# Two feed-forward couples of the last batch but one moved to the last steps, with other row buffers and new order seeds

## The chip, the cores and the metric

The kernel runs on one core of a Trainium2 chip. The metric is the device time of one execution in microseconds (us). The engines of a core are TensorE (PE, matrix products), VectorE (DVE), ScalarE (ACT), GpSimd (POOL) and SyncE (SP, which issues nearly all DMAs here). Each has its own queue and works through it in order; they wait for each other by semaphores.

## What is computed

One transformer block in float32 on x of shape (8, 1024, 256): attention with 16 heads of 64, then a feed-forward part, each with a layernorm before it and another behind it, ahead of the residual sum. Shortened from the reference:

```python
def attn(x):                       # x already normalised
    q, k, v = (einsum('btc,hcd->bhtd', x, W) for W in (Wq, Wk, Wv))
    scores = einsum('bhtd,bhsd->bhts', q, k) / sqrt(64) + bias   # bias by clipped distance, per head
    w = softmax(where(causal, scores, -inf))
    return concat_heads(einsum('bhts,bhsd->bhtd', w, v)) @ Wp + bp

def ffn(x):                        # x already normalised
    x_prev = shift_by_one_row(x)   # zero for the first row
    xr = mu_r * x + (1 - mu_r) * x_prev
    xk = mu_k * x + (1 - mu_k) * x_prev
    return sigmoid(xr @ W_r.T) * (square(relu(xk @ W_k.T)) @ W_v.T)

x = x + layernorm(attn(layernorm(x)))
x = x + layernorm(ffn(layernorm(x)))
```

## The kernel before, in words

**Tiling.** A batch has 1024 rows: eight tiles of 128, or four *couples* of 256 rows (c = 0 to 3). Heads go in pairs; a *unit* is one batch and one pair of heads, so there are 8 x 8 = 64 units (the unit u = 63 is the last). A unit takes four *steps*, 256 in all; a step makes the scores of two row tiles (`STEPS`: tiles 7 and 1, 6 and 0, 5 and 3, 4 and 2). The scores of tiles 4 to 7 ("long") are made in two parts, each in one of two slots `s` of PSUM; those of tiles 0 to 3 ("short") and all other products take one or two of four PSUM banks `pm`.

**The stages of attention.** `do_scores` (L1015): products of k and q in 64x64 tiles of the array (L1041), bias and maximum on DVE (L1070, L1078), exponentials on ACT (L1098), scaling of the probabilities p by the reciprocal of their sum on POOL (L1186). `turn` (L1197): DVE transposes p in 32x32 blocks into `blocks` (L1207); `shuffle` (L1260): sixteen DMAs on SP's queue bring the blocks to their places in `d`, once for each of a unit's two groups of row tiles. `do_av` (L1275): products of d and v (L1293); group 0 holds couples 3 and 0, group 1 couples 2 and 1; ACT saves them to `oT` (L1316). For the last tiles of unit 63 PE transposes p itself (`turn_by_pe`, L1221) and ACT and DVE copy it to d. `do_qk`, `do_v`: projections of the next unit, through the helper `matmul` (L433).

**The rows of a couple.** `stages_in` (L663) loads x rows (`xin`), normalises them (`xn`) and transposes them to `xnT`. `project_out` (L692) multiplies oT by Wp and adds to the rows `y`; `stages_out` (L737) loads the x rows once more (`xre`), normalises y and adds. `stages_ffn` (L752) is the feed-forward part: statistics on DVE (`norm_stats`, L516), normalised rows `yn` (`normed`, L532), transposition to `ynT`, the mixes `xk` and `xr` (one part on ACT, the other on DVE), the products xk by W_k, xr by W_r and ka by W_v (each eight matmuls of 256 columns, L433), relu and tanh on ACT, square, gate, layernorm, sum, store.

Transposition goes two ways. For all batches but the last, `by_dma` (L606): DVE transposes blocks into `st`, four DMAs bring them to DRAM (`via`), one brings them back into the rows' own buffer, ACT places them. In the last batch PE transposes (`turned`, L582), and normalisation and sums are done by ACT and DVE instead of POOL (`edge`).

**Buffers.** A `Ring` is a tag with n buffers; the n+1st owner waits until all users of the first are done. Before, `xin`, `xre`, `xn`, `yn`, `st`, `v` and the four `y{c}` have one buffer each. For batches other than the last, ka takes the ring of ynT.

**The order.** No engine's queue is written by hand. Every piece of work is a `Task` with an engine, a cost estimate, a priority and its dependences; `Planner.simulate` (L216) lists the tasks by priority, and each engine's instructions are emitted in that order. A task's priority is its step number (plus a fixed `RANK` for its kind, plus offsets drawn from a seed) times `STEP`. There are 65 `SEEDS` (L95), one for each stretch of 34 us of the planner's clock. Which work belongs to which step is set at the end of the kernel (L1451 to L1512): with end = the step at which a batch's attention ends, the next batch's rows enter at end - 15 + 2c, the out stages at end + 1 and following, and the feed-forward part of couple c at end + 6 + 3c. For batch 6 (the last but one) end is 224, so couples 2 and 3 enter at steps 236 and 239. The parts of the last batch enter at step LAST = 256.

Of the kernel before, what the change touches and what calls it, by code (L numbers as in the profile page):

```python
# [92 lines left out]

STRETCH = 34
SEEDS = (  # L95
    392905, 816692, 244547, 283470, 560662, 39100, 216772, 294259, 588279, 412218,
    371534, 0, 431774, 883409, 180062, 984965, 373709, 0, 0, 0,
    763639, 658110, 822178, 930278, 665013, 718545, 0, 952361, 100832, 846644,
    0, 137572, 647438, 377597, 0, 469262, 83528, 641677, 323164, 611824,
    444950, 813510, 452093, 622742, 919130, 335621, 0, 751616, 573689, 0,  # L100
    0, 99909, 466380, 402426, 0, 986219, 146830, 82811, 0, 0,
    151578, 369797, 955240, 0, 0,
)


# [47 lines left out]
class Planner:  # L153
# [13 lines left out]
    def add(  # L167
        self,
        eng,
        cost,  # L170
        fn,
        *deps,
        w=(),
        r=(),
        prio=0.0,
        mode="cols",
        banks=0,
        frees=None,
        mb=0.13,
    ):  # L180


        t = Task(eng, cost, fn, prio, mode, banks, mb)
        t.deps = list(deps)
        if self.gate is not None:
            t.deps.append(self.gate)
        for b in r:
            b, part = b if isinstance(b, tuple) else (b, None)
            t.deps += [d for p, d in b.writers if part is None or p == part]
            b.users.append(t)  # L190
        for b in w:
            b, part = b if isinstance(b, tuple) else (b, None)
            if b.maker is None:
                b.maker = t
                t.makes.append(b)
                if b.old is not None:
                    t.deps.append(b.old.users)
                if b.before is not None:
                    t.after.append(b.before.maker)
            elif b.maker is not t:  # L200
                t.after.append(b.maker)

            if frees is not None and b.old is not None:
                frees[0].deps.append(b.old.users)
            if frees is not None and b.maker is not t and (frees[0], 0) not in b.maker.frees:
                frees[0].after.append(b.maker)
            b.writers.append((part, t))
            b.users.append(t)
        if frees is not None:
            t.deps.append(frees[0])  # L210
            t.frees.append(frees)
            frees[0].readers[frees[1]] += 1
        self.tasks.append(t)
        return t
# [143 lines left out]
def tile_attn_ffn_block(  # L358
# [17 lines left out]
    B, T, C = x.shape  # L376
    H, _, D = Wq.shape
# [37 lines left out]
    ins = ctx.enter_context(tc.tile_pool(name="ins", bufs=1))  # L415
    acts = ctx.enter_context(tc.tile_pool(name="acts", bufs=1))
# [12 lines left out]
    def matmul(dst, lhs, rhs, first, last):  # L429
# [5 lines left out]
    rows2 = [P, 2, C]  # L435
    R = {
        "xin": Ring(ins, rows2, "xin", 1),
        "xre": Ring(ins, rows2, "xre", 1),
        "wq": Ring(ins, [P, NC, P], "wq", 1),
        "wk": Ring(ins, [P, NC, P], "wk", 1),  # L440
        "wv": Ring(ins, [P, 2, NC, D], "wv", 1),
        "xn": Ring(acts, rows2, "xn", 1),
        "st": Ring(acts, [P, NQ, 2 * NC, QD], "st", 1),
        "via": Ring(dram, [P, NQ, 2 * NC, QD], "via", 2),
        "yn": Ring(acts, rows2, "yn", 1),
        "xkr": Ring(acts, [P, NC, CT], "xkr", 1),
        "xr": Ring(acts, [P, NC, CT], "xr", 1),
        "ynT": Ring(acts, [P, NC, CT + 1], "ynT", 1),
# [15 lines left out]
        R[n, "long"] = Ring(small, [P, 2, 2], f"{n}_long", 3)  # L464
    for c in range(NCP):
        R["oT", c] = Ring(acts, [P, CT], f"oT{c}", HP + 1)
        R["y", c] = Ring(acts, rows2, f"y{c}", 1)
    for g in range(2):
        R["xnT", g] = Ring(acts, [P, NC, HB], f"xnT{g}", 2)


    def rows_of(t, b, c):
        return t[b, c * CT : (c + 1) * CT, :].rearrange("(n p) c -> p n c", p=P)
# [132 lines left out]
    def by_dma(dst, view, src, what, prio, last):  # L606


        st, via = R["st"](f"st_{what}"), R["via"](f"via_{what}")
        add(  # L610
            "dve",
            0.6,
            lambda: nc.vector.transpose(
                st.tile.rearrange("p r a j -> p a r j"),
                src.tile.rearrange("p k (c r j) -> p (k c) r j", r=NQ, j=QD),
            ),
            r=[src],
            w=[st],
            prio=prio,
        )  # L620


        def leave():
            v = via.tile
            n = 2 * NC * QD
            for q in range(NQ):
                nc.sync.dma_start(
                    bass.AP(
                        tensor=v.tensor,
                        offset=v.offset + q * n,  # L630
                        ap=[[NQ * n, QD], [QD * NQ * n, NQ], [1, n]],
                    ),
                    st.tile[q * QD : (q + 1) * QD],
                )

        def flat(t):
            return t.rearrange("p k f -> p (k f)")

        add("sp", NQ * ISSUE, leave, r=[st], w=[via], prio=prio, mb=0.26)
        add(  # L640
            "sp",
            ISSUE,
            lambda: nc.sync.dma_start(
                flat(src.tile), via.tile.rearrange("p q a j -> p (q a j)")
            ),
            r=[via],
            w=[src],
            prio=prio,
            mb=0.26,
        )  # L650

        def place():
            blks = flat(src.tile).rearrange("p (q k c j) -> p k q c j", k=2, c=NC, j=QD)
            for cc in range(NC):
                nc.scalar.copy(
                    view(dst.tile)[:, cc, :].rearrange("p (k q j) -> p k q j", k=2, j=QD),
                    blks[:, :, :, cc, :],
                )

        add("act", 0.7, place, r=[src], w=[dst], prio=last)  # L660
# [76 lines left out]
    def stages_out(b, c):  # L737


        def s0(prio):  # L740
            project_out(b, c, range(HP, NPAIR) if b < B - 1 else [NPAIR - 1], prio)
            rn = norm_stats(ys[b, c], f"ao_{b}_{c}", prio)
            xre = R["xre" if b < B - 1 else {0: "xre", 3: "xin", 1: "xn", 2: "xre"}[c]](
                f"xre_{b}_{c}"
            )
            load_rows(xre, b, c, prio)
            normed(ys[b, c], ys[b, c], rn, f"ao_{b}_{c}", prio + 1, edge=b == B - 1)
            plus(ys[b, c], xre, prio + 1, edge=b == B - 1)

        return [s0]  # L750

    def stages_ffn(b, c):  # L752

        box = {}

        def buf(name, tag, spare):

            if b < B - 1:
                return R[tag](f"{name}_{b}_{c}")
            return R[spare](  # L760
                f"{name}_{b}_{c}", lambda t: t[:, : NC * CT].rearrange("p (k f) -> p k f", k=NC)
            )
# [2 lines left out]
            box["rn"] = norm_stats(ys[b, c], f"y_{b}_{c}", prio)  # L765

        def s1(prio):
            box["yn"] = buf("yn", "yn", ("p", "short")) if c % 2 else R["yn"](f"yn_{b}_{c}")
            normed(box["yn"], ys[b, c], box["rn"], f"y_{b}_{c}", prio, edge=b == B - 1)

        def s2(prio):
# [557 lines left out]
    def start_lists(lists, prio, lag):  # L1329
        n = max(len(s) + i * lag for i, s in enumerate(lists))  # L1330
        for j in range(n):
            for i, s in enumerate(lists):
                if 0 <= j - i * lag < len(s):
                    s[j - i * lag](prio)
# [7 lines left out]
    with tc.tile_pool(name="prep", bufs=1) as prep:  # L1342
# [16 lines left out]
        for c in range(NCP):  # L1359
# [12 lines left out]
            prio=-4,  # L1372
# [6 lines left out]
            prio=-4,  # L1379
# [8 lines left out]
            prio=-1,  # L1388
# [16 lines left out]
        for half in range(2):  # L1405
# [7 lines left out]
            prio=2,  # L1413
# [30 lines left out]
    LAST = NU * NS  # L1444
    ahead = {}

    def later(step, stages):
        for i, s in enumerate(stages):
            ahead.setdefault(step + i, []).append(s)

    for b in range(B):  # L1451
        end = (b + 1) * NPAIR * NS
        mid = end - HP * NS
        for i, c in enumerate((0, 3, 1, 2)):
            later(mid + 3 + i, [lambda prio, b=b, c=c: project_out(b, c, range(HP), prio)])
        if b + 1 == B:
            for i, c in enumerate((0, 3, 1, 2)):
                later(
                    end - NS + i,
                    [lambda prio, b=b, c=c: project_out(b, c, range(HP, NPAIR - 1), prio)],  # L1460
                )
        else:
            for i, c in enumerate((0, 3, 1, 2)):
                later(end + 1 + 2 * i, stages_out(b, c))
            for c in range(NCP):
                ffn = stages_ffn(b, c)
                later(end + 6 + 3 * c, [lambda prio, ffn=ffn: start_lists([ffn], prio, 1)])
                later(end - 15 + 2 * c, stages_in(b + 1, c))

    for m in range(LAST):  # L1470
        u, st = divmod(m, NS)
# [34 lines left out]
    b = B - 1  # L1506
# [48 lines left out]
```

## Time and profile before

| | |
|---|---|
| three runs | 2192.37, 2194.66 and 3990.92 us; median 2194.66 |
| profiled execution | 2193.71 us, its span 2191.9 us |
| instructions in the span | 61295 |
| busy: PE | 2161.1 us |
| busy: DVE | 1970.5 us |
| busy: POOL | 1526.8 us |
| busy: ACT | 1377.4 us |
| DMA: read from HBM, written to HBM | 59.91 MB, 25.29 MB |
| mean granted TensorE clock | 0.998 |

The span runs from the first to the last instruction of the profiled execution; its own time is 1.8 us longer. A line of the timeline gives the start in us, the time to the end of the merged piece, the engine, the line of the kernel, what was written from what, the shape, the number of records and, in brackets, the idle time before it and what ended it. One float32 matmul of the program is two records on PE. The ends of matmuls are modelled, so the distance from start to next start says more than the length.

### The profile page before, as it was taken

The numbers are of one execution on the slowest core, as the hardware profiler recorded it, in microseconds if no ns is written. First come the engines' busy times: TensorE is split into PE (matmuls) and PEld (weight loads), VectorE is DVE, ScalarE is ACT, GpSimd is POOL, SyncE is SP. The second block draws the span as 40 slices with busy tenths as digits, with TensorE's granted clock in tenths as the row PEclk, the third lists the DMA queues.
The fourth block names the chain that finished last, engine by engine and source line by source line (L and its number), as shares of the span: only waits on it lengthen the run. The fifth ranks groups of instructions, "written<-read, shape, count | busy, mean of one in ns | idle before, by whom it ended". The sixth has DMA issues, their size and how long they took to land.

```text
span 2191.9 us, 61295 instructions
## 1 busy us (share of the span) xinstructions
PE 2161.1 (99%) x21312; PEld 1182.6 (54%) x21312; DVE 1970.5 (90%) x4460; ACT 1377.4 (63%) x4314; POOL 1526.8 (70%) x3709
## 2 busy tenths in 40 slices
PE   7999999999999999999999999999999999999997
PEld 3455555555555555555555555555555555555565
DVE  5998999999998999998999989899889998999776
ACT  5665756666566565665656666565666756667454
POOL 4666677766786768775687766777667775687553
PEclk9999999999999999999999999999999999999999
DMA  5887877867778687776877777777787868877560
GB/s 166 193 199 184 194 175 179 202 167 181 178 179 200 166 193 177 183 189 169 196 180 188 181 189 181 170 175 192 170 190 178 198 167 198 193 177 189 131 152 25
DMA packets 272596, 388.92 MB, mean 177 GB/s; under 512 B 142624, under 2 KB 199968, under 8 KB 272160
## 3 DMA queue, kind: packets, MB, share of 16 engines
q1 hardware_dynamic: 272144, 384.87, 73.3%
q8 instruction: 170, 2.79, 0.6%
q14 instruction: 138, 1.13, 0.2%
q10 hardware_dynamic: 144, 0.14, 0.0%
HBM read 59.91 MB, written 25.29 MB: 39 GB/s over the span
## 4 chain that ended last, share of the span: by engine, by line
PE 89%; DVE 5%; DMA 1%; POOL 1%; issue 1%; ACT 1%; SPq 1%; ACTq 0%; DVEq 0%; POOLq 0%
PE pm L433 46%; PE pm L1293 21%; PE s L1041 16%; PE pm L1041 6%; DVE blocks L1207 2%; DVE nmax L1078 2%; POOL p L1186 1%; SPq L1267 1%; ACT p L1098 0%; DMA d<-blocks 0%; DVE pm L1070 0%; DMA out_dram<-r 0%; DVE s L1070 0%; DMA tab<-in_L_attn_rel_table_dram 0%; DVE y L722 0%
## 5 line engine op out<-in xcount | busy, mean ns | idle before, releaser
L1186 POOL TENSOR_SCALAR p<-p,rcp 128x512 f32<-128x512 f32 (+5 forms) x1536 | 883.9, 595 | 86.0 <-DVE rcp L1165 62.7
L1098 ACT ACTIVATE p<-s,nmax 128x512 f32<-128x512 f32 (+3 forms) x1024 | 616.0, 607 | 398.4 <-DVE nmax L1078 317.4
L1207 DVE STREAM_TRANSPOSE blocks<-p 128x256 f32<-128x256 f32 (+2 forms) x1016 | 724.2, 749 | 50.6 <-POOL p L1186 41.6
L1078 DVE TENSOR_REDUCE nmax<-s 128x2 f32<-128x1024 f32 (+3 forms) x512 | 516.7, 1009 | 33.3 <-PE s L1041 30.1
L1293 PE MATMUL pm<-d,v 128*64 128x256 f32 (+1 forms) x5120 | 523.5, 359 | 0.3 <-DMA d<-blocks 0.3
L1293 PEld LDWEIGHTS pm<-d,v 128*64 128x64 f32 x5120 | 351.8, 137 | 219.4 <-issue 39.6
L1041 PE MATMUL s<-k,q 64*64 64x512 f32 (+3 forms) x4096 | 444.3, 519 | 5.9 <-ACT p L1098 5.7
L1098 ACT ACTIVATE p<-pm,nmax 128x256 f32<-128x256 f32 (+3 forms) x512 | 270.9, 531 | 94.5 <-DVE nmax L1078 68.9
L433 PEld LDWEIGHTS pm<-wv,xnT 128*64 128x64 f32 x4096 | 226.5, 137 | 52.0 <-issue 26.9
L433 PE MATMUL pm<-wv,xnT 128*64 128x128 f32 x4096 | 248.1, 274 | 0.0
L433 PE MATMUL pm<-xnT,wk 128*64 128x512 f32 x1024 | 245.5, 600 | 0.1
L1078 DVE TENSOR_REDUCE nmax<-pm 128x1 f32<-128x256 f32 (+3 forms) x512 | 242.1, 478 | 3.4
L433 PE MATMUL pm<-xnT,wq 128*64 128x512 f32 x1024 | 244.7, 599 | 0.0
L433 PE MATMUL pm<-wp_sb,oT 128*64 128x256 f32 x2048 | 240.5, 381 | 0.7 <-ACT oT L1316 0.7
L1041 PEld LDWEIGHTS s<-k,q 64*64 64x64 f32 x4096 | 133.6, 132 | 180.2 <-issue 95.2
L1098 ACT ACTIVATION_READ_ACCUMULATOR p<-s,nmax 128x1 f32 x1024 | 206.7, 202 | 0.0
L433 PEld LDWEIGHTS pm<-wp_sb,oT 128*64 128x64 f32 x2048 | 141.6, 137 | 101.7 <-issue 25.2
L1041 PE MATMUL pm<-k,q 64*64 64x256 f32 (+3 forms) x2048 | 188.4, 438 | 0.0
L1070 DVE TENSOR_TENSOR pm<-pm,bm 128x144 f32<-128x144 f32 (+1 forms) x512 | 135.3, 298 | 38.1 <-PE pm L1041 36.9
L1140 POOL TENSOR_TENSOR rcp<-nmax 128x2 f32<-128x2 f32 x256 | 51.0, 199 | 148.5 <-DVE nmax L1078 119.0
L1155 POOL TENSOR_TENSOR tot<-tot,rcp 128x4 f32<-128x4 f32 x256 | 52.1, 203 | 146.8 <-ACT rcp L1148 139.8
L433 PEld LDWEIGHTS pm<-xnT,wq 128*64 128x64 f32 x1024 | 68.0, 137 | 129.7 <-issue 104.4
(103 smaller groups left out, 2266.2 us busy)
## 6 DMA issues: line engine op xcount, KB each, us to landing
d<-blocks SPq DMA_DIRECT2D x2032, 144.0 KB, 2.6
xin<-in_L_attn_x_dram SPq DMA_DIRECT2D x32, 256.0 KB, 3.0
wq<-in_L_attn_Wq_dram SPq DMA_DIRECT2D x128, 64.0 KB, 2.2
wk<-in_L_attn_Wk_dram SPq DMA_DIRECT2D x128, 64.0 KB, 2.2
wv<-in_L_attn_Wv_dram SPq DMA_DIRECT2D x64, 128.0 KB, 2.9
xre<-in_L_attn_x_dram SPq DMA_DIRECT2D x32, 256.0 KB, 3.0
out_dram<-r SPq DMA_DIRECT2D x32, 256.0 KB, 2.2
via_in<-st_in SPq DMA_DIRECT2D x112, 64.0 KB, 1.9
```

The source lines that it names most:

```text
L433: nc.tensor.matmul(dst[rows], lhs[:, rows], rhs, start=first, stop=last)
L1041: nc.tensor.matmul(s(hh)[o : o + D], q.tile[rows, tb * P + o : tb * P + o + D], k.tile[rows, c0:c1], start=True, stop=True,)
L1070: nc.vector.tensor_tensor(dst, dst, src, ALU.add)
L1078: nc.vector.tensor_reduce(nmax.tile[:, i, h0:h1], sl.tile[:, :, : c1 - c0] if sl else s(h0), AX.X, ALU.max, negate=True,)
L1098: nc.scalar.activation(ps[hh].tile[:, c0:c1], s(hh), AF.Exp, bias=nmax.tile[:, i, hh : hh + 1], scale=1.0, accum_out=tot.tile[:, i, hh : h ...
L1140: nc.gpsimd.tensor_tensor(rcp.tile[:, 0, :], m1, m0, ALU.subtract)
L1155: nc.gpsimd.tensor_tensor(tot.tile, tot.tile, rcp.tile, ALU.mult)
L1186: nc.gpsimd.tensor_scalar(p, p, rcp.tile[:, i, hh : hh + 1], 1.0, ALU.mult, ALU.mult)
L1207: nc.vector.transpose(blocks[g][:, :, s0 : s0 + 2 * tb + 1 : 2, hh, :].rearrange("p r a j -> p a r j"), p.tile[:, :n].rearrange("p (a r j) ...
L1267: nc.sync.dma_start(d.tile[r * QD : (r + 1) * QD, q].rearrange("p s h j -> p (s h j)"), blocks[g][q * QD : (q + 1) * QD, r].rearrange("p s ...
L1293: nc.tensor.matmul(dst, v[:, jt, rows], src, start=(jt == 0), stop=(jt == 2 * k + 1),)
```

## The change

Three things are done together.

- The feed-forward parts of couples 2 and 3 of batch 6 enter at steps 250 and 253 (`LAST - 6 + 3 * (c - 2)`) and no longer at 236 and 239.
- The rows y of couples 2 and 3 have two buffers each, so that batch 7's rows can be begun while batch 6's are still needed. In return the rings `xre` and `yn` go: the x rows loaded again use `xin`, the normalised rows of the feed-forward part use `xn`. In the last batch the x rows of couples 0, 1, 2 and 3 go to `xin`, `st`, `v` and `xin` (before: `xre`, `xn`, `xre`, `xin`); `st` and `v` are taken as flat rows.
- All 65 seeds are new, so every engine's order changes nearly everywhere.

No instruction is added, removed or changed in shape. The diff, without the list of seeds and with the helper `flat` moved up:

```diff
 SEEDS = (
-    392905, 816692, 244547, 283470, 560662, 39100, 216772, 294259, 588279, 412218,
...
+    87077, 486655, 913775, 923135, 468664, 830281, 0, 100961, 446615, 668238,
...
 )
     R = {
         "xin": Ring(ins, rows2, "xin", 1),
-        "xre": Ring(ins, rows2, "xre", 1),
...
-        "yn": Ring(acts, rows2, "yn", 1),
...
-        R["y", c] = Ring(acts, rows2, f"y{c}", 1)
+        R["y", c] = Ring(acts, rows2, f"y{c}", 1 + c // 2)
...
+    def flat(t):
+
+        names = ("a", "b", "c", "d")[: len(t.shape) - 1]
+        return t.rearrange(f"p {' '.join(names)} -> p ({' '.join(names)})")
...
-            xre = R["xre" if b < B - 1 else {0: "xre", 3: "xin", 1: "xn", 2: "xre"}[c]](
-                f"xre_{b}_{c}"
+            xre = R["xin" if b < B - 1 else ("xin", "st", "v", "xin")[c]](
+                f"xre_{b}_{c}",
+                lambda t: t
+                if t.shape[1] == 2
+                else flat(t)[:, : 2 * C].rearrange("p (n c) -> p n c", c=C),
             )
...
-            box["yn"] = buf("yn", "yn", ("p", "short")) if c % 2 else R["yn"](f"yn_{b}_{c}")
+            box["yn"] = buf("yn", "xn", ("p", "short")) if c % 2 else R["xn"](f"yn_{b}_{c}")
...
             for c in range(NCP):
                 ffn = stages_ffn(b, c)
-                later(end + 6 + 3 * c, [lambda prio, ffn=ffn: start_lists([ffn], prio, 1)])
+
+                at = end + 6 + 3 * c if b + 2 < B or c < 2 else LAST - 6 + 3 * (c - 2)
+                later(at, [lambda prio, ffn=ffn: start_lists([ffn], prio, 1)])
                 later(end - 15 + 2 * c, stages_in(b + 1, c))
```

## The prediction

> **What bounds the kernel now.** I read the page first, then who waited for whom on PE, then three stages by themselves, then PE's and DVE's timelines in the last stage. The page:
>
> ```profile
> PE 2161.1 (99%) x21312; PEld 1182.6 (54%) x21312; DVE 1970.5 (90%) x4460; ACT 1377.4 (63%) x4314; POOL 1526.8 (70%) x3709
> ...
> PE 89%; DVE 5%; DMA 1%; POOL 1%; issue 1%; ACT 1%; SPq 1%; ACTq 0%; DVEq 0%; POOLq 0%
> ```
>
> TensorE (PE) is busy for 2161.1 of 2191.9 us and carries 89% of the chain that ended last. A busy row can hide a slow PE, so I looked at the starts of the matmuls. This is one stretch of PE's timeline, and below it two lines of an earlier one:
>
> ```profile
> 1011.15 1.89 PE L433 MATMUL pm<-xnT,wk 128*64 128x512 f32 x8
> 1012.97 0.88 PE L1041 MATMUL s<-k,q 64*64 64x384 f32 x8
> 1013.77 1.94 PE L433 MATMUL pm<-xnT,wk 128*64 128x512 f32 x8
> ...
> 1023.23 1.94 PE L433 MATMUL pm<-xnT,wq 128*64 128x512 f32 x8
> 1025.00 1.89 PE L433 MATMUL pm<-xnT,wk 128*64 128x512 f32 x8
> 1026.71 1.89 PE L433 MATMUL pm<-xnT,wq 128*64 128x512 f32 x8
> ```
>
> ```profile
> 65.70 0.82 PE L1041 MATMUL s<-k,q 64*64 64x384 f32 x8
> 66.34 0.82 PE L1041 MATMUL pm<-k,q 64*64 64x384 f32 x8
> ```
>
> From start to next start, eight 128x512 records take 1.71 us (1025.00 to 1026.71) when nothing changes, 1.77 just after scores (64*64 tiles), 1.82 just before scores; scores of 384 take 0.64 among scores and 0.80 alone. A trip into scores and back so costs 0.11 + 0.16 + 0.06 = 0.33 us. Everything else runs at a fixed pitch, so PE's work is a constant plus the number of trips. What is left are waits:
>
> ```profile
> 8.00:100.00 92.00, 86.22 (x778) 41.64 (x778) 70.08 (x155) 61.23 (x184) 49.06 (x132) 0.98 0.69 177
> 100.00:2099.00 1999.00, 1994.59 (x19656) 1086.98 (x19656) 1833.83 (x4121) 1268.67 (x4015) 1431.75 (x3473) 1.00 0.76 182
> 2099.00:2192.00 93.00, 80.25 (x888) 53.94 (x880) 63.90 (x175) 46.00 (x115) 40.83 (x95) 0.96 0.31 77
> ```
>
> First number after the comma is PE's busy time, the last but two the granted clock. Idle: 8.0 us before the first matmul, 5.8 to 100 us, 4.4 in the 1999 us of the middle, 12.75 in the last stage, of which 9.3 lie after the last matmul (2182.6 to 2191.9). If all other idle went, 13.6 us would be gained. The last stage:
>
> ```profile
> 2146.74 4.06 PE L1293 MATMUL pm<-d,v 128*64 128x256 f32 x40
> 2151.45 1.95 PE L433 MATMUL pm<-wp_sb,oT 128*64 128x256 f32 x16 [0.65 <-ACT oT L1316]
> 2153.23 1.04 PE L433 MATMUL pm<-ident,yn 128*64 128x128 f32 x16
> 2156.60 3.32 PE L433 MATMUL pm<-xk,wkT 128*64 128x256 f32 x16 [2.33 <-DVE xk L842]
> 2159.71 2.36 PE L433 MATMUL pm<-wrT,xr 128*64 128x256 f32 x16
> 2161.90 1.04 PE L433 MATMUL pm<-ident,yn 128*64 128x128 f32 x16
> ```
>
> PE never waits from 2050 until the last AV (probabilities times v, L1293) at 2146.74. Then it waits 0.82 us by starts (2146.74 + 3.89 of AV, to 2151.45), 0.05, and 2.50 (2154.10 to 2156.60): 3.37 in all, for the serial chain of couple 0 of the last batch. The window 2156.60 to 2161.90 has a granted clock of 0.68: xk and xr products took 3.11 and 2.19 where later ones take 1.73, so the wait cost 1.84 more.
>
> **The change part by part.**
>
> *Work.* By the instruction orders of both programs each engine keeps its count and shapes. Only order and buffers change.
>
> *Seeds.* PE's order is the same up to 86 us, then differs everywhere. Trips into scores: 285 before, 288 after. 3 x 0.33 = **+1.0 us**, wholly on the path. [...]
>
> *Waits of the middle.* They come where a PSUM slot is retaken soon after its last use. I summed PE's pitches over both orders and counted retakes within 3.5 us (long scores), 3.7 (short scores), 3.2 (xk, xr) or 3.0 (ka) of the last user's end, from 100 to 2100 us: 22 before (4, 18, 0, 0), 26 after (10, 8, 5, 3). By the 4.4 us that 22 cost, 26 cost 5.2: **+0.8**. Below: all vanish, -4.4. Above: each of the ten long-score retakes waits 2.14 us, the longest wait of a score for ACT in the profile (70.46 us): +17. I take +0.8, since the kinds and numbers are near those of before.
>
> *Ring sharing.* xre rows now use xin's one buffer, even yn rows xn's. xin's last use for a batch comes at step end-7, xre's first at end+1 (yn's first 13 steps behind xn's last); a step is 2192/256 = 8.6 us, so eight steps, some 69 us, lie between. An xre load lands in 3.0 us. For the last batch SP still loads couple 0's xre long before (its place on SP's queue moves by two rows). Couple 3's load now waits for couple 0's add, couple 2's for the last AV to release v. Both are needed some 7 us later, and a load takes 3.0 (at most 4.9): **0**. If that cover were gone, DVE would stand at couple 3's add, ahead of xk of couple 0, for up to those 4.9 us. The second y buffers add no wait.
>
> *Couples 2 and 3 of batch 6.* Their six products (6 x 1.73 = 10.4 us of PE) leave the stretch at 2010 to 2045, where PE never waits, so all behind comes 10.4 us earlier; and they return before the last AV, where PE never waited either. That is zero so far, if their inputs are in time. I walked PE's new queue, with zero at the AV of unit 62, group 1 (2119.16 before): AV 3.89, v 1.75, projections 2.59, transposes 0.87, v 1.75, xk and xr of couple 2 3.45, transposes 1.31, ka of couple 2 1.73, transposes 2.18, projections 2.59, AV 3.89, transposes 3.27: xk of couple 3 is reached at 29.3. Its rows go by DMA. DVE ends unit 63's block transposes at 3.9 (scores end at 0, then 0.5 bias, 1.9 maxima, 0.95, and what queues). The shuffle's 16 issues take 10.4 (10.27 to 11.52 for 16 in SP's timeline); couple 3's four DMAs stand behind them (1.9, landing 1.9), then the one back (0.3, 2.9): 21.4. ACT copies and multiplies 1.7: 23.1; it then saves the AV that ends at 26.0, multiplies for xk until 27.5, DVE copies 0.5 and gives xk's first half at 28.5. PE waits for nothing, with 0.8 us to spare. **0**, until the DMAs are some 2.5 us late.
>
> *The chain of couple 0.* The new work stands in its way. Zero is now the end of couple 0's last projections (2143.70 before). PE's queue from there: ka of couple 3 1.73, AV 3.89, couple 3's projections 0.86, four more 1.73: couple 0's transposes are reached at 8.2. The chain: normalised by ACT 4.0 (2143.70 to 2147.69), plus x 0.7, statistics 1.24: 5.95. POOL should now take rs_y, but its queue holds couple 3 of batch 6: r at 2.6, statistics 3.85, power 0.95, two scalings of 0.556, an add of 1.28: free at 7.2. Then 0.7 + 0.2 + ACT 1.09 and hops: 9.5. PE waits 1.3 (0.05 before). The 0.82 goes, because couple 3's projections now cover the copy of oT. DVE's queue ahead of xk: couple 3's adds end at 7.05, then an add, 1.24 of statistics, three adds, two more statistics, couple 3's plus 0.7: 12.9, xk's first half at 13.4. PE ended the transposes at 10.4: it waits 3.0. Together 4.3 against 3.37: **+0.95**. From xk to the end the order is the same: 2191.9 - 2156.6 = 35.3 either way, with the 1.84 of low clock in it.
>
> *The clock.* By the row (2.33 idle, then 1.84 lost) a wait of 3.0 loses about the same; so did 2.14 idle at 70.46 (the next product took 2.98 instead of 1.71), while 1.49 at 43.93 and 1.56 at 416.34 lost nothing, so 1.3 does not. [...]
>
> *Sum.* 2193.7 (the profiled execution, span 2191.9 and 1.8 around it; the median of three is 2194.66, 1.0 above) + 1.0 + 0.8 + 0 + 0.95 = **2196.4 us**.
>
> **The rivals.**
> - *The moved products fill the end, as they were placed to.* If couple 3's rows come so late that its products fall beside the chain while PE's queue is still ahead of it, or the chain is quicker than my hops, the 3.37 and the 1.84 go: 2193.7 + 1.0 + 0.8 - 5.2 = 2190.3; with the middle's waits gone too, 2185. Against: all six stand ahead of the last AV in PE's order.
> - *The new order waits more in the middle.* Ten quick retakes of long-score slots at 2.14 each, while DVE is at 48.35 of 50 us in plain stretches (1150 to 1200): 2193.7 + 1.0 + 17 + 0.95 = 2212.7. It decides from about 2 us in all. To leave the 2% it needs 44 us, more than all 26 retakes at 1.6 each.
> - *Couple 3's DMAs are late.* Landing at most 4.8 where 2.9 is the median, 3.8 where 1.9 is: 3.8 late, 1.3 past the 2.5: 2197.7, and with a lost clock 2199.5. That is the slower side by one mechanism, deciding from 2.5 us late.
> - *The change does nothing.* Trips alone, 2194.7.
>
> **How the numbers follow.** Forecast with its neighbours (nothing, late DMAs), 2193 to 2200: 0.50. Filled end or fewer waits, 2184 to 2193: 0.26. More waits, 2200 to 2213: 0.20. Beyond: 0.04, half of it past 2238.6, 2% over the median. Faster by 2% would be under 2150.8; with every wait gone 2193.7 - 13.6 - 1.84 and the low clock before 100 us (2 us) leave 2176, so 0.005. 2% is about what a measurement of this kernel can tell from no change. Range 2186 to 2209.
>
> **What would show it.** Trips: no row of its own, but PE busy up by about 1. Middle: PE idle of 100 to 2099 near 5. Tail: a wait for yn near 1.3, one for xk near 3, none for oT, then xk at 3.1 us instead of 1.73; no wait at couple 3's xk. The forecast is wrong if the middle idles over 10 us, if yn or xk waits under 1 us, or if an xre load releases anyone.

## The result, and the profile after

| | before | after |
|---|---|---|
| median | 2193.21 us (12 runs) | 2196.23 us (12 runs, 2193.71 to 2201.78) |
| profiled execution, its span | 2193.71, 2191.9 us | 2195.71, 2193.9 us |
| ratio after / before | | 1.0017, 95% interval [1.0009, 1.0025] |

One run of the kernel before (3990.92 us) lies outside all others and is left out of the ratio. The medians differ by 3.0 us, and the ratio of the runs puts the cost at 0.17%; 2196.4 us was forecast.

The first line of the page of the kernel after:

```profile
PE 2160.9 (98%) x21312; PEld 1181.2 (54%) x21312; DVE 1964.2 (90%) x4460; ACT 1375.7 (63%) x4314; POOL 1517.2 (69%) x3709
```

PE is busy as long as before. The three stretches of the kernel after (from:to, length, then the busy time of PE, PEld, DVE, ACT, POOL; the last but two is the granted clock):

```profile
8.00:100.00 92.00, 84.61 (x782) 41.27 (x784) 72.32 (x159) 61.09 (x184) 50.17 (x133) 1.00 0.69 178
100.00:2099.00 1999.00, 1994.88 (x19649) 1082.99 (x19645) 1824.02 (x4105) 1267.28 (x4017) 1414.82 (x3465) 1.00 0.76 182
2099.00:2192.00 93.00, 81.36 (x888) 56.95 (x884) 65.93 (x193) 45.83 (x113) 47.10 (x101) 0.97 0.34 86
```

PE idles 4.12 us in the middle, 4.41 before. Up to 100 us PE's order is nearly the same in both, yet 1.6 us of busy time are missing here, and the clock is 1.00 for 0.98. The reason is in PE's timeline:

```profile
70.90 0.77 PE L1044 MATMUL s<-k,q 64*64 64x320 f32 x8 [2.14 <-ACT p L1101]
71.60 1.94 PE L433 MATMUL pm<-xnT,wk 128*64 128x512 f32 x8
73.36 1.89 PE L433 MATMUL pm<-xnT,wq 128*64 128x512 f32 x8
```

The same stretch before:

```profile
70.46 0.77 PE L1041 MATMUL s<-k,q 64*64 64x320 f32 x8 [2.14 <-ACT p L1098]
71.16 3.21 PE L433 MATMUL pm<-xnT,wk 128*64 128x512 f32 x8
74.14 2.36 PE L433 MATMUL pm<-xnT,wq 128*64 128x512 f32 x8
```

The same wait of 2.14 us was followed by slow products in one execution and by quick ones in the other. The granted clock tells why. Up to the last matmul it is half from 71.68 to 75.09 and from 2157.22 to 2160.63 before, and from 2158.53 to 2161.94 after: 3.41 us each time, and the two starts of before lie 2085.54 us apart, 611 steps of 3.413. Two such steps around this wait, before:

```profile
68.27:71.68 3.41, 1.27 (x16) 0.45 (x14) 3.41 (x7) 2.10 (x7) 2.76 (x9) 1.00 1.02 237
71.68:75.09 3.41, 3.41 (x12) 0.97 (x10) 3.41 (x8) 1.30 (x4) 3.19 (x9) 0.50 0.76 171
```

and after:

```profile
66.18:69.59 3.41, 2.14 (x28) 0.57 (x20) 3.41 (x9) 2.68 (x8) 2.68 (x5) 1.00 0.81 196
69.59:73.00 3.41, 2.10 (x16) 0.75 (x18) 3.41 (x8) 1.33 (x5) 2.66 (x9) 1.00 0.94 220
```

Before, the idle time fell into one step, which left PE busy for 1.27 us of it, and the next step has half the clock. After, it fell on two steps, with 2.14 and 2.10 us of work, and the clock stayed at 1.00. Where the steps lie differs from one execution to the next (edges at 71.68 before, at 69.59 and 73.00 after): the kernel before with filler at its end (below) has the same order here and quick products (clock 1.00 and PE busy for 69.75 us up to 85 us, where before has 0.98 and 71.22). So this is luck and no part of the change, and I divided the span at two products that both have, the scores at 85 us and the first AV of the last unit. After:

```profile
85.00 0.98 PE L1044 MATMUL s<-k,q 64*64 64x448 f32 x8
```

and before:

```profile
86.25 0.98 PE L1041 MATMUL s<-k,q 64*64 64x448 f32 x8
...
2137.63 4.06 PE L1293 MATMUL pm<-d,v 128*64 128x256 f32 x40
```

PE's timeline of the last stage of the kernel after:

```profile
2134.10 4.06 PE L1296 MATMUL pm<-d,v 128*64 128x256 f32 x40
2137.99 3.44 PE L433 MATMUL pm<-ident,p 128*64 128x128 f32 x60
2141.27 1.90 PE L433 MATMUL pm<-xk,wkT 128*64 128x256 f32 x16
2142.99 1.90 PE L433 MATMUL pm<-wrT,xr 128*64 128x256 f32 x16
...
2145.80 1.90 PE L433 MATMUL pm<-wvT,ka 128*64 128x256 f32 x16
2147.53 4.06 PE L1296 MATMUL pm<-d,v 128*64 128x256 f32 x40
2151.42 2.76 PE L433 MATMUL pm<-wp_sb,oT 128*64 128x256 f32 x24
2154.94 1.15 PE L433 MATMUL pm<-ident,yn 128*64 128x128 f32 x16 [0.76 <-ACT yn L559]
2158.90 3.43 PE L433 MATMUL pm<-xk,wkT 128*64 128x256 f32 x16 [2.81 <-DVE xk L845]
2162.16 1.89 PE L433 MATMUL pm<-wrT,xr 128*64 128x256 f32 x16
2163.89 1.04 PE L433 MATMUL pm<-ident,yn 128*64 128x128 f32 x16
```

Couple 3's three products (2141.27, 2142.99, 2145.80) stand ahead of the last AV, and PE waits for none of them. The wait for oT is gone; there is one for yn (0.93 by starts) and one for xk (3.09), and xk and xr together take 4.99 where 3.46 is usual: 1.53 for the low clock. It is again one step, before and after:

```profile
2157.22:2160.63 3.41, 3.41 (x20) 1.85 (x20) 3.05 (x10) 1.71 (x4) 2.71 (x5) 0.50 0.02 5
```

```profile
2158.53:2161.94 3.41, 3.04 (x15) 1.71 (x17) 3.34 (x11) 1.12 (x4) 3.33 (x5) 0.50 0.01 2
```

Half of PE's 3.41 and 3.04 us in it is 1.7 and 1.5, close to the 1.84 and 1.53 by which the products are longer.

| stretch (us) | before | after | difference |
|---|---|---|---|
| start to the scores at 85 | 86.25 | 85.00 | -1.25 |
| from there to the first AV of unit 63, without couple 3's 5.18 | 2046.20 | 2049.10 | +2.90 |
| that AV to the last matmul, with couple 3's 5.18 | 50.18 | 50.51 | +0.33 |
| last matmul to the end | 9.27 | 9.29 | +0.02 |

The sum is 2.00, the difference of the spans.

### The profile page after: what moved, and what is told of

The parts are those of the page before. It is cut to its first block, busy times and chain, and to the rows that moved or that the text cites. A ratio compares the mean times of both kernels' runs of the same rounds, so it can differ in the third digit from the quotient of the medians.

```text
span 2193.9 us, 61305 instructions
## 1 busy us (share of the span) xinstructions
PE 2160.9 (98%) x21312; PEld 1181.2 (54%) x21312; DVE 1964.2 (90%) x4460; ACT 1375.7 (63%) x4314; POOL 1517.2 (69%) x3709
## 5 line engine op out<-in xcount | busy, mean ns | idle before, releaser
L1210 DVE STREAM_TRANSPOSE blocks<-p 128x256 f32<-128x256 f32 (+1 forms) x1016 | 726.1, 754 | 50.2 <-POOL p L1189 43.5
L1044 PE MATMUL s<-k,q 64*64 64x512 f32 (+3 forms) x4096 | 449.4, 521 | 6.7 <-ACT p L1101 6.4
L1319 ACT COPY oT<-pm 128x256 f32<-128x256 f32 x256 | 88.4, 377 | 90.8 <-PE pm L1296 89.7
```

The source lines that it names most:

```text
L1044: nc.tensor.matmul(s(hh)[o : o + D], q.tile[rows, tb * P + o : tb * P + o + D], k.tile[rows, c0:c1], start=True, stop=True,)
L1210: nc.vector.transpose(blocks[g][:, :, s0 : s0 + 2 * tb + 1 : 2, hh, :].rearrange("p r a j -> p a r j"), p.tile[:, :n].rearrange("p (a r j) ...
L1319: lambda: nc.scalar.copy(o.tile.rearrange("p (t q j) -> p t q j", t=2, j=QD), pm(t, i)[:, :CT].rearrange("p (q t j) -> p t q j", t=2, j=QD),),
```

## The experiments

All but the two rows that begin with "before" start from the kernel after. The kernel before was timed beside them (2193.10, 2192.85 and 2193.14 us in the three groups of runs).

| run | median us | ratio to before, 95% interval |
|---|---|---|
| filler in couple 0's wait | 2194.61 | 1.0007 [0.9998, 1.0016] |
| own ring for the x rows | 2196.24 | 1.0015 [1.0006, 1.0024] |
| old seeds | 2261.66 | 1.0320 [1.0302, 1.0338] |
| couples 2, 3 at the old steps | 2198.62 | 1.0029 [1.0018, 1.0041] |
| before with the new seeds | 2257.54 | 1.0291 [1.0275, 1.0307] |
| couple 3's products later | 2194.12 | 1.0010 [1.0001, 1.0019] |
| two adds on POOL | 2196.81 | 1.0021 [1.0012, 1.0030] |
| both of these | 2196.59 | 1.0018 [1.0009, 1.0027] |
| couple 3's rows late | 2205.55 | 1.0052 [1.0038, 1.0065] |
| 43 more trips | 2212.38 | 1.0088 [1.0074, 1.0101] |
| later products, filler for couple 1 | 2194.99 | 1.0010 [1.0001, 1.0019] |
| before with the filler | 2190.83 | 0.9991 [0.9982, 1.0000] |

**What a trip into scores costs.** The edit, in the AV:

```diff
                 d, v, acc = dd[u, g].tile, qkv[u, "v"].tile, pm(t, i)
+                if i == 0 and u < NU - 1:
+                    nc.tensor.matmul(acc[:D, :8], ident[:D, :D], ident[:D, :8], start=True, stop=True)
```

> The changed kernel, with one product of a 64x64 tile and 8 columns ahead of each AV of the first 63 units (126 products, overwritten by the AV). 83 of them stand behind scores and change nothing; 43 stand between products of 128x64 tiles, so TensorE goes into the other tiling and back 43 times more: 331 trips for 288. Theory (a trip costs 0.33 us as read from the starts): 43 x 0.33 = 14.2, and 126 x 0.01 for the products: 2196.2 + 15.4 = 2211.6, down to 2208 where waits of the middle go. Rival (half of the 0.33 belongs to the scores themselves, a change costs about 0.09): 43 x 0.18 + 1.3: 2205. Rival (changes are hidden by the pipelining of the products): 2197 to 2198.

It took 2212.38 us, 16.2 more than the kernel after. PE's timeline of this run, at one added product that stands between 128x64 tiles and one behind scores:

```profile
1125.24 1.89 PE L433 MATMUL pm<-xnT,wq 128*64 128x512 f32 x8
1127.06 0.28 PE L1288 MATMUL pm<-ident 64*64 64x8 f32 x2
1127.27 4.11 PE L1298 MATMUL pm<-d,v 128*64 128x256 f32 x40
...
1147.74 0.82 PE L1044 MATMUL s<-k,q 64*64 64x384 f32 x8
1148.38 0.23 PE L1288 MATMUL pm<-ident 64*64 64x8 f32 x2
1148.54 4.11 PE L1298 MATMUL pm<-d,v 128*64 128x256 f32 x40
```

The wq product takes 1.82 to the next start (1.71 or 1.72 among its like), the added one 0.21, and the AV behind it 0.05 more: about 0.36 with the small product in it. Behind scores the way to the AV is 0.16, where without the added product it is 0.12. 43 x 0.36 + 83 x 0.04 = 18.8; the idle time of the middle falls from 4.12 to 0.99, which gives 3.1 back: 15.7, for 16.2 measured. The price of 0.33 agrees with that, 0.36 with the small product in it; three trips are 1 us.

**Whether the shared ring costs anything.** The x rows get a ring of their own again:

```diff
+        "xre": Ring(ins, rows2, "xre", 1),
...
-            xre = R["xin" if b < B - 1 else ("xin", "st", "v", "xin")[c]](
+            xre = R["xre" if b < B - 1 else ("xre", "st", "v", "xin")[c]](
```

> The changed kernel with a ring of its own for the x rows that are loaded again (couples 0 of the last batch too), instead of xin's. PE's order is the same as in the changed kernel to the end. Theory: the shared buffer costs nothing, since eight steps lie between its owners: within 1 us of the changed kernel, PE idle of 100 to 2099 us at 4 to 5 us in both. Rival: loads of x rows come late with the shared buffer and hold POOL's and DVE's queues: 2 us or more are won.

2196.24 us, the time of the kernel after. Sharing costs the x rows nothing that these runs can tell. The normalised rows, which share xn's ring, were not run apart.

**The seeds.** The kernel after with the list of seeds of before, and the kernel before with the new list:

> The changed kernel with the old seeds. Its PE order has 320 trips into scores and back (288 in the changed kernel). Theory: a trip costs 0.33 us and the waits are nearly those of the changed kernel: 32 x 0.33 = 10.6 us more than the changed kernel, 2204 to 2209, with PE's busy time up by 10. Rival: seeds only shuffle work under a PE that is full anyway, and the time is within 2 us of the changed kernel; or the old seeds fit their buffers so badly that waits of the middle grow from 4 to over 15 us.

> The kernel before with the new seeds and nothing else. TensorE's order has 317 trips into scores and back where the kernel before has 285. Theory (the seeds were fitted to the buffers and the steps, and fit nothing else; the changed kernel with the old seeds took 2261.7 us, of which 10 were trips and 55 waits for scores' slots): 32 trips x 0.33 = 10.6 and waits of several tens of us, 2230 to 2265. Rival (the new seeds are as good in either structure, and only the trips count): 2193.1 + 10.6 = 2204, up to 2210.

2261.66 and 2257.54 us. The first expectation took trips for nearly all of it and fell; its rival was right. PE's waits (us in total, times, longest) with the old seeds in the kernel after:

```profile
PE s L1044 <- ACT p L1101: 30.8, 32, 2.8
```

and in the kernel after itself:

```profile
PE s L1044 <- ACT p L1101: 6.4, 6, 2.1
```

With the wrong list, scores wait 32 times for a slot that ACT has not left, where they waited 6 times; in the kernel before with the new list they wait 29 times, 32.2 us in total. Either list is worth some 65 us, but only with the buffers and steps that it was found for. "New seeds" is therefore no part of this change that could be had alone, and the +1.0 of the trips is the remainder of two large effects that nearly cancel: 285 trips become 320 with the new structure and the old list, and 288 with the new list.

**The move alone.** With the old steps for couples 2 and 3 (`at = end + 6 + 3 * c`):

> The changed kernel, but couples 2 and 3 of batch 6 enter where they did before (steps 236 and 239). PE's order differs from the changed kernel only behind 1963 us; trips 293 (288). Theory: the move gives nothing, since its products land ahead of the last AV: 5 x 0.33 = 1.7 more for trips, about 1 less at the end, so 2196 to 2198. Rival: the move fills idle PE, and without it the time is 3 to 5 us above the changed kernel's, 2200 or more, with PE waiting over 5 us behind the last AV.

2198.62 us, 2.4 above the kernel after. The two intervals overlap, so that the move is worth something within the new structure is likely and not shown. PE makes 5 more trips in this run's trace (293), which are 1.7 us by the price above, and the wait for oT (0.78) is back.

**How late couple 3's rows may come.** The four DMAs out are issued six times over:

```diff
-            for q in range(NQ):
+            for q in list(range(NQ)) * (6 if what == f"y_{B - 2}_3" else 1):
```

> The changed kernel, with the four DMAs that carry couple 3's normalised rows of batch 6 out issued six times over: 20 more issues of 0.49 us, so the rows come back 9.9 us later; the order of every engine stays. Theory (the prediction's step: these DMAs cost nothing until they are some 2.5 us late, and then all of it; in the trace of the changed kernel ScalarE has 3.75 us between its work on the rows and its next step for xk, and VectorE's xk ends 0.4 to 0.8 before TensorE takes it): TensorE waits 5 to 6.5 us for couple 3's xk, and with a low clock behind it loses up to 1.7 more: 2201 to 2205. Rival (the end waits for VectorE and not for these products, so most of the delay is swallowed there): 2196 to 2198.

2205.55 us, 9.3 more, and a little above the 2201 to 2205 of the theory. In this run's timelines SP's 24 issues take 13.84 us where the four took 1.97, so the rows are 11.9 late. PE then stands here:

```profile
2137.22 1.48 PE L433 MATMUL pm<-ident,p 128*64 128x128 f32 x24
2146.17 3.67 PE L433 MATMUL pm<-ident,p 128*64 128x128 f32 x36 [7.47 <-ACT oT L1319]
2149.67 1.89 PE L433 MATMUL pm<-xk,wkT 128*64 128x256 f32 x16
```

and ACT's timeline tells why:

```profile
2144.34 0.71 ACT L655 COPY ynT<-yn 128x256 f32<-128x256 f32 x2 [13.67 <-DMA yn<-via_y]
2144.96 0.90 ACT L817 ACTIVATE xr<-ynT,onem 128x256 f32<-128x256 f32 x2
2145.77 0.62 ACT L1319 COPY oT<-pm 128x256 f32<-128x256 f32 x2
```

PE waits 7.6 by starts (2137.22 + 1.31 to 2146.17) and the slow clock adds 1.5 to the transposes behind it. 11.9 - 7.6: the rows may be 4.3 late, where the prediction had 2.5. And the first to suffer is not xk, but the AV's two PSUM banks: ACT waits for the rows with the copies of oT queued behind, and PE's transposes want those banks. The danger was real, and the kernel after stays 4 us clear of it.

**Whether products can fill the end.** Couple 3's later stages are put back by 12 in priority, couple 0's first:

```diff
-            ynT = box["ynT"] = R[("xnT", c // 2) if b == B - 1 and c % 2 else "ynT"](
+            ynT = box["ynT"] = R[("xnT", c // 2) if b == B - 1 and c != 2 else "ynT"](
...
+        stages = [s0, s1, s2, s3, s4, s5, s6, s7, s8, s9]
+        if (b, c) == (B - 2, 3):
+            stages[5:] = [lambda prio, s=s: s(prio + 12) for s in stages[5:]]
...
-        start_lists([stages_ffn(b, c)], LAST + 0.1 * c, 1)
+        start_lists([stages_ffn(b, c)], LAST + (0.1 * c if c else -10), 1)
```

> The changed kernel, with couple 3's products of batch 6 put later: xr behind the last AV, ka behind couple 0's transposes, and couple 0's projections 3.45 us of products earlier; couple 0's transposed rows get another buffer. Theory A (the waits of the end are a serial chain that more products of TensorE can cover): the wait for yn (0.93) goes, the one for xk falls from 3.09 to under 1, and the low clock behind it (1.53) goes with it: 2196.2 - 4.5 = 2191.7, between 2190.5 and 2193. Theory B (the end is bound by VectorE, which has no gap from 2152 to 2162): the waits come back at xr or at couple 1's products, 2195 to 2197.

Median 2194.12 us, between the ranges of the two theories; its interval overlaps that of the kernel after. PE's timeline:

```profile
2159.32 1.95 PE L433 MATMUL pm<-xk,wkT 128*64 128x256 f32 x16 [0.88 <-DVE xk L845]
2161.10 1.90 PE L433 MATMUL pm<-wrT,xr 128*64 128x256 f32 x16
2163.46 1.95 PE L433 MATMUL pm<-wvT,ka 128*64 128x256 f32 x16 [0.46 <-DVE ka L882]
2165.23 1.04 PE L433 MATMUL pm<-ident,yn 128*64 128x128 f32 x16
2167.46 1.15 PE L433 MATMUL pm<-ident,yn 128*64 128x128 f32 x16 [1.18 <-ACT yn L559]
2169.84 3.47 PE L433 MATMUL pm<-xk,wkT 128*64 128x256 f32 x16 [1.23 <-DVE xk L845]
```

Couple 0's wait for yn is gone and the one for xk is 0.88, as theory A has it. But the waits return at ka, at the next yn and at couple 1's xk, with a low clock behind. From the first AV of unit 63 to the last matmul it is 50.67 us, for 50.51: theory B in this trace. (This execution took 2199.75 us, the longest of its eleven, but by the time up to that AV.) DVE works without a gap from 2154.6 to 2166 in it.

**Taking work off VectorE.** The adds of couples 2 and 3 go to POOL:

```diff
-            plus(ys[b, c], xre, prio + 1, edge=b == B - 1)
+            plus(ys[b, c], xre, prio + 1, edge=b == B - 1 and c not in (2, 3))
```

> The changed kernel, with the residual adds of couples 2 and 3 of the last batch on GpSimd (1.27 us each) in place of VectorE (0.69 each); one of them stands ahead of couple 0's xk in VectorE's queue. Theory B (VectorE's queue sets xk): xk comes 0.7 earlier, the wait of 3.09 is 2.4, and the low clock costs as much or a little less: 2195.0 to 2195.7. Theory C (xk is set by ScalarE's copy of the transposes and its multiply, which end 0.2 to 0.7 before VectorE reaches xk): 2196.2, no change.

> Both of the edits before together. Theory A: the waits are gone with the later products alone, and this adds nothing: 2190.5 to 2193, equal to the run before it but one. Theory B: only both together take the wait for xk away, 2192 to 2194 and 1 us or more below either alone. In theory C the adds on GpSimd delay xr of couple 0, whose two scalings stand behind them in GpSimd's queue: 2193 to 2196.

2196.81 us alone, 2196.59 with the later products: nothing, or a loss. In the first run couple 0's xk does come 3.33 us behind its transposes and no longer 3.96, 0.6 where theory B foresaw 0.7; the end stage is nevertheless 52.19 long. In the second it is 51.85. POOL's adds can hold up DVE's smallest work, as the timeline of the second shows:

```profile
2157.35 1.27 POOL L574 TENSOR_TENSOR y<-y,xre 128x512 f32<-128x512 f32 x1 [1.21 <-ACT y L559]
2157.39 1.25 DVE L529 TENSOR_SCALAR mv_y<-mv_y 128x2 f32<-128x2 f32 x1
```

An instruction on two numbers a partition, 0.17 in the median of the kernel after, takes 1.25 and ends 0.02 behind POOL's add. The kernel after has two more such places: at 1122.92 and 1395.12 the same instruction takes 1.18 and 1.22 and ends 0.02 and 0.03 behind an add of POOL's. So an add of 0.69 taken from DVE can cost it 1.1 (1.25 less 0.17).

**What the low clock costs.** Ten pairs of products that nobody reads are put behind couple 0's transposes in the kernel after, and nine (the 36 records below, not ten pairs as the expectation says) in the kernel before. The edit in the kernel after:

```diff
+            if warm:
+                for _ in range(10):
+                    matmul(warm.tile[:, 0, :P], ident, ident, True, True)
```

> The changed kernel with ten pairs of 128x128 dummy products behind couple 0's transposes of the last batch (2.2 us of extra PE work into a free PSUM slot; the results are not touched), so that PE idles some 0.6 us and not 2.81 before xk of couple 0. Theory A (as the prediction priced it): the low clock behind the wait costs about 1.5 us (2158.90 to 2162.16 is 3.26, where 1.73 is normal), so xk's product takes 1.73 again and the time falls by 1.5 us against the changed kernel. Theory B: the next start, the transposes of couple 1 at 2163.89, hangs on DVE's, POOL's and ACT's chain for couple 1's rows and not on PE, so the product gets shorter and PE then waits: time within 0.4 us of the changed kernel. In both, xk starts 3.96 us after the transposes, as now.

> The kernel before, with ten such pairs behind couple 0's transposes, ahead of its wait of 2.33 us for xk. Theory (the low clock behind that wait costs the kernel before 1.84 us, as in the sum): xk and xr take 1.73 each, 2193.0 - 1.84 = 2191.2. Rival (VectorE's next rows come no earlier, and the products only wait for them instead): 2192.5 to 2193.5.

2194.61 us in the kernel after (1.6 below it), 2190.83 in the kernel before (2.3 below it, and the lowest of all). In both traces the granted clock is 1.00 from 2099 to 2180. PE's timeline in the kernel before with the filler:

```profile
2150.49 1.04 PE L433 MATMUL pm<-ident,yn 128*64 128x128 f32 x16
2151.36 2.13 PE L433 MATMUL warm<-ident 128*64 128x128 f32 x36
2153.86 2.05 PE L433 MATMUL pm<-xk,wkT 128*64 128x256 f32 x16 [0.36 <-DVE xk L846]
2156.67 1.95 PE L433 MATMUL pm<-wrT,xr 128*64 128x256 f32 x16 [0.76 <-DVE xr L846]
2158.45 1.04 PE L433 MATMUL pm<-ident,yn 128*64 128x128 f32 x16
```

xk comes no earlier (3.37 behind the transposes, as without filler) and is short, but then PE waits 0.8 for DVE's xr. From one couple's transposes to the next it is 7.96, for 8.67 without filler: 0.7 of the 1.84 comes back. In the kernel after it is 8.63 for 8.95. The medians moved more than these two traces. Without filler the low clock also lasts longer in some executions: 10.23 in the run with its own ring, where xr took 2.82 as well. The mean granted clock of the runs points the same way: 0.9967 over the twelve runs of the kernel after and 0.9981 over the eleven with filler; 0.9976 over the 70 runs of the kernel before that were timed beside the experiments and 0.9984 with filler. That this makes up the rest is likely; no trace here shows it.

For couple 1 in the kernel with the later products:

> The kernel with couple 3's products put later, with ten pairs of 128x128 products that nobody reads behind couple 1's transposes, where TensorE waited 1.18 for the next rows, 1.23 for xk, and then ran two products at about half clock (3.25 and 1.94 by starts where 1.73 is usual). Theory: the idle time is broken up, both products take 1.73, and 1.7 us go: 2194.1 - 1.7 = 2192.4. Rival (VectorE sets the pace, and waits come back as in the run of the chain of couple 0 with the same filler): 2193.5 to 2194.5.

2194.99 us. In its trace both products take 1.78 and 1.73 and the end stage is 48.98, 1.7 shorter, as the theory has it; the median does not show it (2194.12 without). The start alone varies by more: the scores at 85 us came at 84.2 to 88.6 in the eight traces that share PE's order up to there. So this stays open.

## Why the prediction was right, point by point

- *Trips, +1.0.* Right, and the price is measured by the 43 added trips. The row named to show it, PE's busy time up by 1, did not: it fell by 0.2, since the low clock at 71 us of the kernel before lengthens its products by 1.7 (the 1.25 of the table, and 0.44 that the kernel after was behind by then).
- *Waits of the middle, +0.8.* The step that failed in its method. More slots are retaken quickly (26 for 22), yet PE idles 4.12 for 4.41; and in the eight traces that share the new order up to the last unit the idle time is 1.9 to 4.1 (mean 3.2), in two traces of the old order 2.1 and 4.4. Counting retakes does not foretell it. Between the two products that bound the middle these eight traces take 2048.1 on average (2046.5 to 2049.2), the two of the old order 2045.4: +2.7. The trips are 1.0 of it. The other 1.7 stands in no wait that the profile lists and remains unexplained; that it comes near the 0.8 is luck. Part of it can be delays that only the starts show: at 677.10 in the kernel after, wq takes 2.04 to the next scores where 1.82 is usual, and no wait is listed. How many such places there are was not measured.
- *Ring sharing, 0.* Right; shown for the x rows by the run with its own ring.
- *Couples 2 and 3 of batch 6, 0.* Right. PE took couple 3's xk at 2141.27 without a wait; DVE's two halves had ended 0.8 and 0.4 before, where 0.8 was worked out. The slack of the DMAs was put too low, 2.5 for 4.3, and the wait would have come at the PSUM banks and not at xk.
- *The chain of couple 0, +0.95.* The mechanism was right in each part: the wait for oT goes, one for yn appears (0.93 for 1.3), xk waits 3.09 (3.0). PE takes yn as soon as ACT's first half (0.59) is done, where the whole (1.09) was reckoned; POOL was free even 0.3 later than worked out. With the low clock at 1.53 for 1.84 it comes to +0.33.
- *The low clock, alike on both sides.* Nearly right for the two profiled executions (1.53 for 1.84 at the end), but the rule behind it was wrong: the prediction went by the length of a wait, and the same 2.14 us of wait were followed by half the clock before and by the full one after; in the step of 3.41 us ahead of each half-clock stretch PE was busy for at most 1.59 (last section). It is also not quite alike over all runs. Runs of equal mean granted clock differ by less than the medians do: at 0.998 they took 2194.89 us on average after (4 runs) and 2192.43 before (38 of the 70), at 0.997 2195.44 (3) and 2193.60 (23). So some 0.5 to 1.2 of the 3.0 us go with the clock; whether the new order or chance brings that, these runs can't tell. As a price of 1.84 that filler would bring back it is too high in the traces: DVE's xr is late by itself, and 0.3 and 0.7 came back, where the medians moved by 1.6 and 2.3.
- *Its own signs of being wrong.* Two of them came up: yn's wait of 0.93 is under 1 us, and an x load did release POOL once, for 0.6 us. The second is no effect of the change (twice and 1.6 us before, once and 0.6 with the own ring). The first says that the chain was quicker than worked out.
- *Rivals.* The filled end was put at 2190.3; when the products were put there on purpose, the waits went on to the next couple. Late DMAs were a real danger, 4 us away.

So the mechanism was right and the sum in part by luck: of the +2.7 that was forecast and the +3.0 of the medians, the end gave 0.6 less than worked out, and the middle 1.7 where 0.8 was put.

No work was removed from PE, which is busy 98% of the time; six products changed places with others inside a stretch where PE never waits, the waits at the end hang on DVE and POOL, and the new order costs a little more than the old.

## What to carry to other kernels

Work moved towards a stall fills it only if it stands behind the last thing that PE does before the stall; and if the stall belongs to another engine's queue, it moves on to the next couple. A seed found by search is part of the buffers and steps that it was found with: judge the two together, and never one change at a time. Compare two executions between products that both have, so that luck at the start does not count as an effect.

## What the runs showed of the hardware

- The granted clock changed in steps of 3.41 us, and the steps at half clock came behind steps in which PE was busy for little: 1.27, 1.08 and 0.97 us in the kernels before and after (the waits there were 2.14, 2.33 and 2.81 us long), and not behind 2.10 and 2.14 us. Behind the first 12 us and up to the last matmul, every other step of these two traces had PE busy for at least 1.50 us. I divided all fourteen traces into such steps, from the edges of their half-clock stretches. Of some 8900 steps at full clock behind the first 12 us, 41 were followed by half the clock; PE was busy for at most 1.59 us in each of them, and for at least 1.39 in all others. So the same 2.14 us without a product were followed by half the clock or by none, by where they fell (the wk products 2.98 by starts before, 1.76 after).
- GpSimd's add over 512 columns can hold up VectorE: its instruction on two columns took 1.25 us for 0.17 and ended 0.02 behind the add. No run here shows which kinds of instructions do this to each other.
- Going into another tiling and back cost 0.33 us in the kernel before, and 0.36 in the run with 43 more trips, where a single small product is all that is done there.
